# Holding back the value sums of every third step in a streamed attention kernel

## The chip, the cores and the metric

The kernel runs on one core of one Trainium2 chip. Times are device microseconds. The time of the kernel is the median of its runs; one further execution was taken with the profiler on, and its own time is given beside its span.

## The reference

Two transformer layers on 2048 rows of 256 features, 16 heads of 16. The first layer splits the rows into two halves: each attends to itself, then each to the other half, then an MLP with gelu. The second layer attends to all 2048 rows with a mask, then to a context of 1601 rows, then an MLP with relu. All four attentions are of this kind:

```
scores = jnp.einsum('bhqd,bhkd->bhqk', q, k) / jnp.sqrt(jnp.float32(hd))
if mask is not None:
    scores = jnp.where(mask == 0, jnp.float32(-1000000000.0), scores)
attn = jax.nn.softmax(scores, axis=-1)
out = jnp.einsum('bhqk,bhkd->bhqd', attn, v)
```

## The kernel before

**Units.** The four attentions are stages 0 to 3 of one stream. A unit is one block of 512 queries with one group of 4 heads; there are 68. A unit's keys come in tiles of 128. For each tile there are two steps, one for each pair of heads: 16 steps a unit in stages 0 and 1, 16 or 32 in the masked stage 2, 26 in stage 3; 1440 steps in all, 928 of them in stages 0, 1 and 3.

**A step** (`stream`, the loop at L1194). In this order PE is given:
- maxima of the next unit (`take_maxima`, L1200, from `maxima`): scores with queries on the partitions (L860, two matmuls that use 64 rows of the array each) into a score tile, which DVE reduces to the maximum (L875; L868 where there's a mask). About one such pair a step in stages 0 and 1; 32 for the 26 steps of a unit in stage 3.
- without a mask, the value sums that are due (L1201 to L1203): one entry of the list `pending`.
- the weights of this step (`second[s2]()`, L1204, from `weights_of`): scores with keys on the partitions (L938), minus the maxima (L945), in the masked stage the mask as well (L953), into a score tile; ACT takes exp of it into a tile `e` (L958).
- with a mask, the value sums come only now (L1205).
- `after(step)`: items with a delay (turning the maxima into rows, L899 to L904; dividing by the sums), transfers, and one piece of the background work.

**Value sums** (`values_of`). For each tile four matmuls (L975; the trace shows each as two) add `V` times `e` into a sum tile `m_ps`, each for one head in 32 columns of the array. The first and the last tile of a unit are summed whole, 512 queries wide, and leave an empty entry (`None`) in the list for the step after; every other tile is summed in two halves of 256 queries, one a step. So there are as many entries as steps. A unit's entries are put on the list in its fourth step (`s2 == 3`), and one is taken in each step; the last three are taken in the first three steps of the next unit. When those are through, `copy_sums` takes the sums out (L1007).

**Tiles.** Score tiles `s_ps` are two PSUM banks each, and there are three (`big_ps`, L107), used in turn by maxima and weights. The sum tiles m0 and m1 are one bank each; the small products of other work use the one that is not in use. `e` has five buffers (`EB`, L55).

**What sets the order.** The order on every engine is the order in which the program issues, fixed when it is built. Projections, MLPs and norms of the blocks run as generators (`chain_self` and so on) in the list `background`: each `yield` gives a number of steps to wait, and the first entry's due time is `background[0][1]`, in steps of `now[0]`. `before` and `after` advance them a piece at a time when they are due.

Of the kernel before, what the change touches and what calls it, by code (L numbers as in the profile page):

```python
# [66 lines left out]
def slot_rows(st, slot):  # L67
    return sum(key_rows(st, n) for n in KEYS[st][slot])


def slots_of(st, b):

    return ((b // 2,), (1 - b // 2,), (0, 1), (0, 1))[st]
# [3 lines left out]
def two_layers(ctx: ExitStack, tc: tile.TileContext, a: dict, out: bass.AP):  # L77
# [585 lines left out]
    now = [0]  # L663
# [30 lines left out]
    def want(*place):  # L694
        waiting.extend((kind, *place) for kind in ("keys", "values"))
# [186 lines left out]
    def negated(u):  # L882

        neg = sb.tile([P, TPB, 2, 2], F32, tag="neg", bufs=2, name="neg")
        nc.vector.tensor_reduce(
            neg.rearrange("p t c i -> p (t c i)"),
            u["pm"].rearrange("p t c i n -> p (t c i) n"), AX.X, ALU.max, negate=True,
        )
        v = negpad.rearrange("p t (c x) -> p t c x", c=2)
        nc.vector.tensor_copy(v[:, :, :, 0:3:2], neg)  # L890
        nc.vector.tensor_tensor(
            v[:, :, :, 1:4:2], neg, v[:, :, :, 0:3:2].bitcast(F32), ALU.subtract
        )

    def as_rows(u):

        m = one_ps()
        for qt in range(TPB):
            nc.tensor.matmul(  # L899
                m[:, qt * P : (qt + 1) * P], lhsT=negpad[:, qt, :], rhs=identR,  # L900
                start=True, stop=True,
            )
        u["nm"] = sb.tile([P, BLK], F32R, tag="nm", bufs=2, name="nm")
        nc.scalar.copy(u["nm"], m)  # L904
        if "part" in u:

            t = sb.tile([P, 2, 4 * BLK // P], F32, tag="mh", bufs=2, name="mh")
            for j in range(4):
                for h in range(2):
                    r = 64 * (j // 2) + 2 * (j % 2) + h  # L910
                    nc.sync.dma_start(
                        t[PH * j : PH * (j + 1), h, :], u["nm"][r : r + 1, :].bitcast(F32)
                    )

            def add():
                n = u["minus"] = part_tile(u, "minus")
                nc.vector.tensor_tensor(n, t[:, 0, :], t[:, 1, :], ALU.add)

            later.append([4, add, False])
# [180 lines left out]
    def stream(stages):  # L1100

        units = []
        for st in stages:
            for b in ORDER[st]:
                blocks[st, b] = {}
                if (st, b) == (2, SPLIT):
                    units += [
                        {"st": st, "b": b, "g": g, "slots": (slot,), "part": slot}
                        for slot in range(2) for g in range(NG)
                    ]  # L1110
                else:
                    units += [
                        {"st": st, "b": b, "g": g, "slots": slots_of(st, b)} for g in range(NG)
                    ]
        for i, u in enumerate(units):
            u["i"] = i

        columns: list = []
        at = 0
        for u in units:  # L1120
            steps = [(slot, kt) for slot in u["slots"] for kt in range(-(-slot_rows(u["st"], slot) // P))]
            if u["st"] == 2 and u["g"] == 0:
                columns += [
                    (at + 2 * n - COLUMNS, u["b"], slot, kt) for n, (slot, kt) in enumerate(steps)
                ]
            u["start"], u["steps"] = at, 2 * len(steps)
            at += 2 * len(steps)

        todo: list = []
        for u, w in zip(reversed(units), [*reversed(units[:-1]), None]):  # L1130
            tiles = maxima(u)
            n = len(tiles)
            begin, length = (w["start"], w["steps"]) if w else (-n, n)
            for k in range(n - 1, -1, -1):
                due = begin + k * length / n - AHEAD
                if u.get("part") == 1 and u["g"] == 0:

                    due = begin + (n - 1) * length / n - AHEAD - (n - 1 - k) * SPACING
                todo.append([min(due, todo[-1][0] - SPACING) if todo else due, u, tiles[k]])

        def take_maxima(step):
            while todo and todo[-1][0] <= step:
                _, u, f = todo.pop()
                f()
                if not todo or todo[-1][1] is not u:
                    all_maxima(u)

        def all_maxima(u):
            negated(u)
            later.append([3, lambda: as_rows(u), True])  # L1150
            if u.get("part") == 0 and u["g"] == NG - 1:
                want(2, 1, 1)

        def before():

            if unfinished and background and not background[0][2] and background[0][1] <= now[0]:
                if not advance(background[0]):
                    background.pop(0)

        def after(step):  # L1160

            now[0] += 1
            due = [x for x in later if x[0] <= 0]
            later[:] = [[x[0] - 1, *x[1:]] for x in later if x[0] > 0]
            for x in due:
                x[1]()
            turned = any(x[2] for x in due)
            while columns and columns[0][0] <= step:
                mask_columns(*columns.pop(0)[1:])
                turned = True  # L1170
            load_ready()
            soon = any(x[0] <= 0 and x[2] for x in later)
            soon = soon or (columns and columns[0][0] <= step + 1)
            if background and background[0][1] <= now[0]:
                if not background[0][2] or not (turned or soon):
                    if not advance(background[0]):
                        background.pop(0)

        streaming[0] = True
        for u in units[:2]:  # L1180
            load_queries(u)
        for step in range(math.floor(todo[-1][0]), 0):
            small[0] = 1
            before()
            take_maxima(step)
            after(step)
        pending: list = []
        step = 0
        for u in units:
            i = u["i"]  # L1190
            masked = u["st"] == 2
            small[0] = i % 2
            second = weights_of(u)
            for s2 in range(len(second)):  # L1194
                before()
                if s2 == 3:
                    pending += values_of(u)
                if s2 == 1 and i + 2 < len(units):
                    load_queries(units[i + 2])
                take_maxima(step)  # L1200
                f = pending.pop(0) if pending else None  # L1201
                if f and not masked:
                    f()  # L1203
                second[s2]()  # L1204

                if f and masked:
                    f()
                after(step)
                step += 1
                if s2 == 2:  # L1210
                    small[0] = (i + 1) % 2
                if s2 == 2 and i:
                    w = units[i - 1]
                    copy_sums(w)
                    part = w.get("part")
                    if part is None:
                        later.append([3, lambda w=w: invert(w), False])
                        later.append([6, lambda w=w: divide(w), False])
                    elif part == 1:
                        v = units[i - 1 - NG]  # L1220
                        later.append([3, lambda w=w, v=v: compare(w, v), False])
                        later.append([4, lambda w=w, v=v: invert_both(w, v), False])
                        later.append([7, lambda w=w: (fetch_first(w), divide(w)), False])
                    if w["g"] == NG - 1 and part != 0:
                        chain_after(w)
        small[0] = len(units) % 2
        for f in pending:
            if f:
                f()
        for x in later:  # L1230
            x[1]()
        flush((0, 1))
        streaming[0] = False
        w = units[-1]
        copy_sums(w)
        invert(w)
        divide(w)
        chain_after(w)
        while background:
            if not advance(background[0]):  # L1240
                background.pop(0)
        flush((None,))
# [92 lines left out]
```

## Time and profile before

| what | us |
|---|---|
| median of 3 runs (3391.25 to 3396.46) | 3392.64 |
| the profiled execution | 3403.53 |
| its span | 3401.7 |
| before the stream's first step (to 131) | 131.0 |
| stage 0 (131 to 632.5): PE busy 465.9 | 501.5 |
| stage 1 (632.5 to 1271.4): PE busy 578.2 | 638.9 |
| stage 2, masked (1271.4 to 2510): PE busy 1191.4 | 1238.6 |
| stage 3 (2510 to 3325): PE busy 766.4 | 815.0 |
| the end (from 3325) | 76.7 |

The stages are cut where the first L938 of each starts. PE's granted clock is 0.97 to 0.99 in all four stages. A line of the timeline gives the start, the duration, engine, source line, operation, what it writes and reads, shapes, a count, and in brackets the idle time of the engine before it with what ended it. PE is the matmul, PEld the weight load; "64*128" is the part of the array that a matmul uses, rows by columns. A matmul's recorded duration reaches past the start of the next one, since matmuls are pipelined, so what a piece of PE's work costs is read from the starts.

### The profile page before, as it was taken

The page shows a single profiled execution, that of the slowest core. Times are in us where ns is not written, and L with a number is a line of the kernel's source. Part 1 is how long each engine was busy: PE and PEld are TensorE (multiplying, and loading weights), DVE is VectorE, ACT ScalarE, POOL GpSimd, SP SyncE. Part 2 cuts the span into 40 slices and gives each one's busy share as a digit, 9 for nine tenths or more (in the row PEclk, how much of TensorE's full clock was granted, in tenths as well). Part 3 has the DMA queues.
Part 4 walks back from the last instruction along what each step waited for, and adds up shares of the span by engine and source line. Part 5 has one row for each costly group of instructions (what it writes and reads, how often), then busy time and mean ns, then how long its engine had stood idle before and what let it go on. Part 6 is the DMA issues. An engine that isn't in the chain of part 4 may idle for free.

```text
span 3401.7 us, 56761 instructions
## 1 busy us (share of the span) xinstructions
PE 3113.2 (92%) x22592; PEld 1362.0 (40%) x22592; DVE 2120.7 (62%) x3858; ACT 1713.7 (50%) x1868; POOL 404.6 (12%) x344
## 2 busy tenths in 40 slices
PE   4799999998999889898999999999999999999995
PEld 2334444444444433333333333343334444444433
DVE  2676766764646455366767777767656747657541
ACT  1265655655545445343555555554546646546461
POOL 0001101101010121104023012201010011110102
PEclk8799999999999999899999999999999999999997
DMA  5652162160204121343111001102241100000000
GB/s 177 140 105 65 36 117 65 48 128 24 65 18 114 32 84 37 94 100 107 51 39 51 15 20 58 32 17 55 49 87 43 26 10 26 25 18 26 10 14 16
DMA packets 162362, 191.20 MB, mean 56 GB/s; under 512 B 82584, under 2 KB 95520, under 8 KB 162096
## 3 DMA queue, kind: packets, MB, share of 16 engines
q1 hardware_dynamic: 162096, 187.57, 22.3%
q8 instruction: 178, 2.92, 0.4%
q14 instruction: 88, 0.72, 0.1%
HBM read 129.91 MB, written 48.46 MB: 52 GB/s over the span
## 4 chain that ended last, share of the span: by engine, by line
PE 51%; DVE 5%; ACT 4%; DMA 2%; SPq 2%; POOL 1%; issue 1%; ACTq 0%; POOLq 0%; DVEq 0%
PE m_ps L975 13%; PE s_ps L938 8%; PE s_ps L860 8%; PE s_ps L953 7%; PE s_ps L945 6%; ACT e L958 3%; PE m_ps L515 2%; DVE s_ps L868 2%; PE m_ps L535 2%; DVE pm L875 1%; PE m_ps L460 1%; DMA raw<-in_mask 1%; PE m_ps L385 1%; DVE t L328 1%; PE m_ps L415 1%
## 5 line engine op out<-in xcount | busy, mean ns | idle before, releaser
L958 ACT ACTIVATE e<-s_ps 128x1024 f32<-128x1024 f32 (+1 forms) x1440 | 1468.1, 1025 | 1375.0 <-PE s_ps L945 794.8
L875 DVE TENSOR_REDUCE pm<-s_ps 128x2 f32<-128x1024 f32 (+3 forms) x1024 | 1120.9, 1106 | 534.7 <-PE s_ps L860 530.2
L975 PE MATMUL m_ps<-e,V 128*32 128x256 f32 (+2 forms) x10432 | 903.6, 418 | 7.3 <-ACT hT L354 4.4
L868 DVE CUSTOM_DVE_ANT_0 s_ps<-s_ps,bias 128x512 f32<-128x512 f32 x1024 | 712.8, 701 | 295.4 <-PE s_ps L860 161.6
L860 PE MATMUL s_ps<-kT,q 64*128 64x512 f32 (+3 forms) x3072 | 676.6, 443 | 111.8 <-ACT e L958 51.1
L938 PE MATMUL s_ps<-q,kT 64*128 64x512 f32 (+1 forms) x2880 | 677.3, 466 | 51.8 <-ACT e L958 28.4
L945 PE MATMUL s_ps<-nm,sel 64*128 64x512 f32 (+1 forms) x2880 | 575.2, 395 | 0.1
L860 PEld LDWEIGHTS s_ps<-kT,q 64*128 64x128 f32 x3072 | 294.1, 186 | 528.1 <-issue 301.1
L938 PEld LDWEIGHTS s_ps<-q,kT 64*128 64x128 f32 (+1 forms) x2880 | 270.5, 184 | 496.6 <-issue 241.0
L975 PEld LDWEIGHTS m_ps<-e,V 128*32 128x32 f32 (+1 forms) x10432 | 206.9, 108 | 433.6 <-issue 415.3
L953 PE MATMUL s_ps<-biasT,ident 128*128 128x512 bf16 x1024 | 311.4, 386 | 0.0
L1053 POOL TENSOR_TENSOR oT<-oT,rd_rows 64x512 f32<-64x512 f32 x64 | 81.7, 1277 | 1904.8 <-DMA rd_rows<-rd_dr 1491.1
L945 PEld LDWEIGHTS s_ps<-nm,sel 64*128 64x128 f32 (+1 forms) x2880 | 275.2, 187 | 12.1 <-ACT nm L904 0.8
L805 POOL TENSOR_SCALAR bias<-raw 128x512 bf16<-128x512 int32 x64 | 123.1, 1924 | 266.4 <-DMA raw<-in_mask 256.4
L868 DVE DVE_READ_ACCUMULATOR2_ANT pm<- 128x1 f32 x1024 | 144.9, 141 | 0.0
L953 PEld LDWEIGHTS <-ident 128*128 128x128 bf16 x1024 | 58.4, 97 | 187.8 <-issue 187.8
L393 DVE SCALAR_TENSOR_TENSOR lo<-m_ps,qkb,hi 128x512 fp32r<-128x512 f32 (+2 forms) x56 | 41.1, 734 | 137.3 <-ACT hi L392 94.3
L535 PE MATMUL m_ps<-w_mlp,hid 128*128 128x256 f32 x448 | 111.4, 405 | 11.9 <-ACT hid L534 11.9
L385 PE MATMUL m_ps<-hT,w_qk 128*128 128x512 f32 (+2 forms) x224 | 109.8, 613 | 9.3 <-DVE lo L393 8.8
L515 PE MATMUL m_ps<-hT,w_mlp 128*128 128x512 f32 x224 | 111.0, 618 | 1.1 <-ACT hT L354 1.1
L535 PEld LDWEIGHTS m_ps<-w_mlp,hid 128*128 128x128 f32 x448 | 86.3, 200 | 36.5 <-ACT hid L534 16.3
L415 PE MATMUL m_ps<-w_v,hT 128*128 128x256 f32 (+1 forms) x212 | 58.0, 420 | 21.8 <-DVE lo L393 21.4
(106 smaller groups left out, 1220.9 us busy)
## 6 DMA issues: line engine op xcount, KB each, us to landing
q<-q_dr SPq DMA_DIRECT2D x544, 64.0 KB
kT<-k_dr SPq DMA_DIRECT2D x192, 128.0 KB
raw<-in_mask SPq DMA_DIRECT2D x64, 256.0 KB
q_dr<-hi SPq DMA_DIRECT2D x32, 256.0 KB
q_dr<-lo SPq DMA_DIRECT2D x32, 256.0 KB
oT<-sums SPq DMA_DIRECT2D x256, 32.0 KB
rd_rows<-rd_dr SPq DMA_DIRECT2D x64, 128.0 KB
v_dr<-v SPq DMA_DIRECT2D x14, 544.0 KB
```

The lines of the kernel that those rows point to most:

```text
L385: nc.tensor.matmul(m[:, :n], lhsT=wqk[:, k, w, c, :], rhs=hT[:, k, :n], start=k == 0, stop=k == 1)
L515: nc.tensor.matmul(m, lhsT=w1[k][:, f * P : (f + 1) * P], rhs=hT[:, k, :], start=k == 0, stop=k == 1,)
L535: nc.tensor.matmul(m[:, q2 * D : (q2 + 1) * D], lhsT=hid[f][:, qt * P : (qt + 1) * P], rhs=w2[f // 4][:, f % 4, :], start=f == 0, stop=f = ...
L805: nc.gpsimd.tensor_scalar(bias_rows[b, slot, qt][:, j * BLK : (j + 1) * BLK], raw, 0.0, MASKED, ALU.is_equal, ALU.mult,)
L860: nc.tensor.matmul(s[:, h, :nn], lhsT=u["q"][64 * h : 64 * h + 64, i, qt * P : (qt + 1) * P], rhs=kT[g][slot][64 * h : 64 * h + 64, i, c : ...
L868: nc.vector.tensor_tensor_reduce(out=s[:, h, :], in0=s[:, h, :], in1=bias_rows[b, slot, qt][:, c : c + nn], scale=1.0, scalar=-3.0e38, op0 ...
L875: nc.vector.tensor_reduce(u["pm"][:, qt, :, i, n], s[:, :, :nn], AX.X, ALU.max)
L938: nc.tensor.matmul(s[:r, h, :], lhsT=kT[g][slot][64 * h : 64 * h + 64, i, kt * P : kt * P + r], rhs=u["q"][64 * h : 64 * h + 64, i, :], st ...
L945: nc.tensor.matmul(s[:r, h, :], lhsT=sel[64 * h : 64 * h + 64, i, :r], rhs=u["nm"][64 * h : 64 * h + 64, :], start=False, stop=not masked,)
L953: nc.tensor.matmul(s[:, h, :], lhsT=ident16, rhs=bias_columns[b, slot, kt], start=False, stop=True,)
L958: nc.scalar.activation(e[:r], s[:r], AF.Exp, scale=SCALE)
L975: nc.tensor.matmul(u["av"][PH * j : PH * (j + 1), cut], lhsT=V[g][slot][:r, kt * GW + j * VW : kt * GW + j * VW + PH], rhs=u["e"][n, j % 2 ...
```

## The change

In stages without a mask, a step whose number is a multiple of three leaves its entry on the list if no piece of background work is due (`quiet`) and at least four steps of the unit are done (`s2 >= 4`). The count `owed` grows by one each step; a step that sums takes as many entries as are owed. So in three steps it is none, then two, then one. If a piece is due, or in the masked stage, or in a unit's first four steps, everything that is owed is summed. The order of maxima, sums and weights in a step is unchanged.

```
         pending: list = []
+        owed = 0
         step = 0
...
                 take_maxima(step)
-                f = pending.pop(0) if pending else None
-                if f and not masked:
-                    f()
+                owed += 1
+
+
+                quiet = not (background and background[0][1] <= now[0])
+                sums = []
+                if masked or not quiet or step % 3 or s2 < 4:
+                    sums = [f for f in pending[:owed] if f]
+                    del pending[:owed]
+                    owed = 0
+                if not masked:
+                    for f in sums:
+                        f()
                 second[s2]()
 
-                if f and masked:
-                    f()
+                if masked:
+                    for f in sums:
+                        f()
                 after(step)
```

## The prediction

> **What bounds the kernel now.** I read the page first: busy time, then the chain that ended last, then the waits of PE, and at last the timeline of the stages that the change touches.
>
> ```profile
> PE 3113.2 (92%) x22592; PEld 1362.0 (40%) x22592; DVE 2120.7 (62%) x3858; ACT 1713.7 (50%) x1868; POOL 404.6 (12%) x344
> ...
> PE 51%; DVE 5%; ACT 4%; DMA 2%; SPq 2%; POOL 1%; issue 1%; ACTq 0%; POOLq 0%; DVEq 0%
> ```
>
> PE leads both. ACT and DVE are far from full, so only their latency can matter, not their throughput. PE's own waits, longest first:
>
> ```profile
> PE s_ps L860 <- ACT e L958: 51.1, 84, 1.2
> ...
> PE s_ps L938 <- ACT e L958: 28.4, 94, 0.9
> ```
>
> The dearest wait is not for data: L860 (maxima scores) reads nothing that L958 (exp) writes. It waits until exp has emptied the score tile that it is to write over; there are three. Now an ordinary stretch of stage 0, PE alone (start us, duration us; idle before it in brackets):
>
> ```profile
> 338.57 0.50 PE L938 MATMUL s_ps<-q,kT 64*128 64x512 f32 x2
> 338.91 0.39 PE L945 MATMUL s_ps<-nm,sel 64*128 64x512 f32 x2
> 339.15 0.39 PE L860 MATMUL s_ps<-kT,q 64*128 64x512 f32 x2
> 339.47 0.64 PE L975 MATMUL m_ps<-e,V 128*32 128x256 f32 x8
> 340.04 0.50 PE L938 MATMUL s_ps<-q,kT 64*128 64x512 f32 x2
> ```
>
> From one L938 to the next, a "row", is 1.47 us with PE never waiting. The same kernel already has rows without values, since the first and last tile of a unit are summed whole and leave the next step empty. Here is one, with what follows:
>
> ```profile
> 360.31 0.50 PE L938 MATMUL s_ps<-q,kT 64*128 64x512 f32 x2
> ...
> 360.65 0.40 PE L945 MATMUL s_ps<-nm,sel 64*128 64x512 f32 x2
> ...
> 360.88 0.40 PE L860 MATMUL s_ps<-kT,q 64*128 64x512 f32 x2
> ...
> 361.12 0.39 PE L938 MATMUL s_ps<-q,kT 64*128 64x512 f32 x2
> ...
> 361.14 1.94 ACT L958 ACTIVATE e<-s_ps 128x1024 f32<-128x1024 f32 x2 [0.91 <-PE s_ps L945]
> 361.35 0.40 PE L945 MATMUL s_ps<-nm,sel 64*128 64x512 f32 x2
> ...
> 362.22 0.49 PE L860 MATMUL s_ps<-kT,q 64*128 64x512 f32 x2 [0.48 <-ACT e L958]
> ...
> 362.65 0.64 PE L975 MATMUL m_ps<-e,V 128*32 128x256 f32 x8
> ...
> 363.22 0.50 PE L938 MATMUL s_ps<-q,kT 64*128 64x512 f32 x2
> ```
>
> The empty row takes 0.81 us, but the next L860 then stands: its tile was filled by the L938 of 360.31, whose exp starts at 361.14 and ends 1.02 us later, and it starts at 362.22, 1.91 us after that L938. So the two rows together take 2.91 us with one half tile, almost what two ordinary rows take with two (2.93). In the timeline all 21 such places of stages 0 and 1 where no piece of other work lies between have that L860 1.90 to 1.92 us after the L938. This is the change's pattern, made by the kernel itself.
>
> **What the Trainium skill says.** "TensorEngine Tiling (Array Packing)", section Tiling Modes: changing the tiling mode drains the array. The trace agrees: a group of four L975 matmuls of 256 columns follows another 0.24 us later, but L938, in the other mode, 0.33 us later. "PSUM — Partial Sum Buffer", section Specifications (TRN2): eight banks of 2 KiB a partition. Three score tiles of two banks and two sum tiles of one fill them, so there's no fourth score tile; the waits above agree. "Perfetto Trace Analysis", section Optimization Strategy: the same gap recurring on the engine that should be full can mean that there's no room for the next tile. The 0.48 us before L860 is such a gap.
>
> **The change part by part.** Walking the new loop, 196 of 928 unmasked steps hold their sums back (103 in stage 3, 93 in stages 0 and 1). In 10 the held entry is an empty one, so 186 places really change. Built, PE's order shows just that: runs of eight L975 where four stood, one instruction stream otherwise; DVE, ACT, POOL and SP keep theirs. A moved half tile issues four matmuls (eight in the trace), no DMA; no queue but PE's is passed. No tile, load or exp is added.
>
> *Switches saved.* A row without its half tile takes 0.81 for 1.47: −0.66. The half tile costs two more groups in the next run: 2 × 0.24 = +0.48. After scores instead of values, L945 follows its L938 in 0.23, not 0.34: −0.11. Together −0.29 us a place, −54 us for 186, if nothing waits.
>
> *Wait added.* The second L860 comes 0.81 + 0.23 + 0.23 = 1.27 us after the first L938, and can't start before 1.91. Behind it on PE stand 16 value matmuls and the next L938; DVE's maximum of that tile starts late too. A weight load that waits isn't ahead of time: L860 to L975 is then 0.43, not 0.32. With a double run of 3 × 0.24 + 0.33 = 1.05 the two rows take 1.91 + 0.43 + 1.05 = 3.39 for 2.93: +0.46. By the other way, 2.91 above and 0.48 more is 3.39 too. Afterwards nothing is late: the second exp ends near 2.9, before its tile is wanted at 3.9; the wait isn't paid back, since PE has no slack in ordinary rows.
>
> I sorted the 186 places by the two rows that they stand in before (durations from the timeline):
> - 66 with two ordinary rows: +0.46, +30 us.
> - 27 in stage 3 with a row of two L860 pairs. 16 where that row loses its values: it waits for exp until 1.91 with or without them, so their 0.48 is simply added, +7.7. In 7 the row that gets them has two pairs: 1.91 + 0.30 (second pair) + 0.30 + 1.05 = 3.56 for 3.33, +1.6. In 4 the next row waits as well, so some 0.3 of the 0.48 stays, +1.2.
> - 17 with one pair each and a row of 1.90 (L938 waits there for the exp just before). In 9 the second row's wait swallows the loss: 0. In 8: 0.47, +3.8.
> - 34 with a row over 2.05 (after an empty row, a DMA or a table load): between −0.29 and +0.46; mostly cover is there; I take +0.1, +3.4.
> - 23 with the turned maxima (L899) in a row: 0.79 us longer, so L860 arrives after 1.91 and the wait vanishes; I take −0.25 of the −0.29: −5.8.
> - 8 at the end with fewer maxima: −0.2, −1.6.
> - 11 beside pieces: −0.29 to +0.46; I take 0.
>
> Sum: 30 + 10.5 + 3.8 + 3.4 − 5.8 − 1.6 = +40 us. The profiled execution took 3403.5 (span 3401.7 and 1.8 around), 0.3% over the median of 3392.6; it would become 3443.8, and the median 3432.9. I name 3433, 1.2% slower.
>
> **The rivals.**
> *Switches win (faster).* The drain is saved everywhere, and the wait at L860 only takes the place of one that came soon after anyway: the 84 and 94 waits above show that score tiles are often late. It decides by the wait a place: under 0.29 us it's a gain, over it a loss. At none it is 3392.6 − 54 = 3339. Against it: 0.64 us (1.91 − 1.27) at every empty row, and 66 ordinary places with no wait to displace.
> *Cover is wider than I see (no change).* If the waits are inherited by the next ones (DMA, L938 behind exp), the 66 places cost nothing and the total is some +10; if the 27 do too, nothing: 3393 to 3411.
> *All stall.* If the 34, 23 and 11 lose 0.46 like the rest, 68 × 0.46 = 31 instead of −2.4: +74, 3466; a further knock-on on chains of pieces would add to it.
> That the change does nothing is excluded by PE's order.
>
> **How the numbers follow.** Forecast 0.70, its own range from the two unknown kinds (45 places, −16 to +17 about what I took) and some 5 us of spread: 3412 to 3455. Inherited waits 0.10, switches win 0.12, all stall 0.08. From 3398 to 3464 keeps eight in ten. A measurement of this kernel can tell about 0.2% (7 us) from no change. Faster than that: 0.11; within it: 0.06; slower: 0.83.
>
> **What would show it.** Right: L860 behind ACT e L958 grows from 84 waits and 51 us to about 180 and 95 (idle shows some 0.48 for a loss of 0.64), and L938 behind it by some 8 us; L975's busy time hardly moves; ACT and DVE do the same work over a longer span; the masked stage keeps its 1239 us; stage 3 grows by some 23 us. Wrong: double runs that follow L860 in 0.32 us with no idle before it, so two rows in 2.64. Then exp is not what L860 waits for.

## The result, and the profile after

The changed kernel takes 3423.7 us (median of 13 runs, 3409.7 to 3430.0) beside 3397.1 for the kernel before on the same chips (13 runs): ratio 1.0073, 95% interval 1.0059 to 1.0086. The change costs 0.7%, some 25 us; 1.2% (40 us) had been forecast.

The page after: busy time and the chain that ended last.

```profile
PE 3078.9 (90%) x22592; PEld 1376.9 (40%) x22592; DVE 2117.8 (62%) x3858; ACT 1704.3 (50%) x1868; POOL 404.6 (12%) x344
...
PE 50%; DVE 6%; ACT 4%; DMA 2%; issue 1%; SPq 1%; POOL 1%; ACTq 0%; POOLq 0%; DVEq 0%
```

PE is busy for 34 us less than before and yet the span is 6 us longer, so PE stands idle for 40 us more. The busy time falls because two single runs of L975 are recorded with 0.64 us each and a double run with 1.07, 0.21 less, which makes 39 us at 186 places. The waits of PE, for the same two instructions as before:

```profile
PE s_ps L860 <- ACT e L958: 81.5, 162, 1.2
PE s_ps L938 <- ACT e L958: 39.6, 78, 1.0
```

L860's wait for exp has gone from 84 times and 51.1 us to 162 times and 81.5 us, L938's from 28.4 to 39.6 us. Here is one held-back place in stage 0 (step 138), PE alone; in the kernel before its two rows took 1.46 and 1.47 us.

```profile
393.09 0.50 PE L938 MATMUL s_ps<-q,kT 64*128 64x512 f32 x2 [0.38 <-ACT e L958]
393.43 0.40 PE L945 MATMUL s_ps<-nm,sel 64*128 64x512 f32 x2
393.67 0.39 PE L860 MATMUL s_ps<-kT,q 64*128 64x512 f32 x2
393.89 0.40 PE L938 MATMUL s_ps<-q,kT 64*128 64x512 f32 x2
394.12 0.39 PE L945 MATMUL s_ps<-nm,sel 64*128 64x512 f32 x2
395.00 0.50 PE L860 MATMUL s_ps<-kT,q 64*128 64x512 f32 x2 [0.49 <-ACT e L958]
395.44 1.07 PE L975 MATMUL m_ps<-e,V 128*32 128x256 f32 x16
396.44 0.50 PE L938 MATMUL s_ps<-q,kT 64*128 64x512 f32 x2
```

The row without values takes 0.80 us; then L860 stands until 395.00, 1.91 us after the L938 of 393.09, the same 1.91 that the empty rows before had. The double run (16 records of L975) comes behind it, and the two rows take 3.35 us.

By stages, from the first L938 of each to that of the next (in stage 3 to its last), the kernel grows by 3.0, −0.4 and −3.0 us in stages 0, 1 and 2 and by 12.9 us in stage 3. The profiled executions differ by less than the medians (3409.7 and 3403.5), and their granted clocks differ with them: 0.973 after and 0.968 before, and 0.005 of 3405 us are 17 us (an estimate). That is why the places are compared by pairs of rows below, and kernels by runs.

### The profile page after: what moved, and what is told of

The parts are those of the page before. It is cut to its first block, busy times and chain, and to the rows that moved or that the text cites. A ratio compares the mean times of both kernels' runs of the same rounds, so it can differ in the third digit from the quotient of the medians.

```text
span 3407.8 us, 56762 instructions
## 1 busy us (share of the span) xinstructions
PE 3078.9 (90%) x22592; PEld 1376.9 (40%) x22592; DVE 2117.8 (62%) x3858; ACT 1704.3 (50%) x1868; POOL 404.6 (12%) x344
## 4 chain that ended last, share of the span: by engine, by line
PE 50%; DVE 6%; ACT 4%; DMA 2%; issue 1%; SPq 1%; POOL 1%; ACTq 0%; POOLq 0%; DVEq 0%
PE m_ps L975 14%; PE s_ps L860 8%; PE s_ps L938 8%; PE s_ps L953 7%; PE s_ps L945 5%; ACT e L958 4%; PE m_ps L515 2%; DVE s_ps L868 2%; PE m_ps L535 2%; DVE pm L875 1%; DMA raw<-in_mask 1%; PE m_ps L460 1%; PE m_ps L385 1%; DVE t L328 1%; POOL bias L805 1%
## 5 line engine op out<-in xcount | busy, mean ns | idle before, releaser
L958 ACT ACTIVATE e<-s_ps 128x1024 f32<-128x1024 f32 (+1 forms) x1440 | 1458.6, 1024 | 1399.7 <-PE s_ps L945 820.6
L875 DVE TENSOR_REDUCE pm<-s_ps 128x2 f32<-128x1024 f32 (+3 forms) x1024 | 1118.5, 1107 | 556.8 <-PE s_ps L860 554.9
L975 PE MATMUL m_ps<-e,V 128*32 128x256 f32 (+2 forms) x10432 | 864.7, 415 | 6.8 <-ACT hT L354 4.4
L860 PE MATMUL s_ps<-kT,q 64*128 64x512 f32 (+3 forms) x3072 | 680.8, 446 | 140.8 <-ACT e L958 81.5
L938 PE MATMUL s_ps<-q,kT 64*128 64x512 f32 (+1 forms) x2880 | 669.0, 460 | 70.0 <-ACT e L958 39.6
L945 PE MATMUL s_ps<-nm,sel 64*128 64x512 f32 (+1 forms) x2880 | 573.1, 393 | 0.1
L860 PEld LDWEIGHTS s_ps<-kT,q 64*128 64x128 f32 x3072 | 291.8, 185 | 576.3 <-issue 303.8
L938 PEld LDWEIGHTS s_ps<-q,kT 64*128 64x128 f32 (+1 forms) x2880 | 269.9, 184 | 464.2 <-issue 203.4
L975 PEld LDWEIGHTS m_ps<-e,V 128*32 128x32 f32 (+1 forms) x10432 | 226.9, 109 | 419.7 <-issue 373.2
L945 PEld LDWEIGHTS s_ps<-nm,sel 64*128 64x128 f32 (+1 forms) x2880 | 274.4, 186 | 13.5 <-ACT nm L904 0.8
L393 DVE SCALAR_TENSOR_TENSOR lo<-m_ps,qkb,hi 128x512 fp32r<-128x512 f32 (+2 forms) x56 | 41.1, 734 | 135.6 <-ACT hi L392 99.2
L385 PE MATMUL m_ps<-hT,w_qk 128*128 128x512 f32 (+2 forms) x224 | 111.5, 622 | 8.6 <-DVE lo L393 8.1
L515 PE MATMUL m_ps<-hT,w_mlp 128*128 128x512 f32 x224 | 111.0, 618 | 1.0 <-ACT hT L354 1.0
L392 ACT ACTIVATE hi<-m_ps,qkb 128x512 fp32r<-128x512 f32 (+2 forms) x56 | 37.8, 675 | 75.4 <-PE m_ps L385 58.5
```

Of the source, the lines that this page charges most:

```text
L385: nc.tensor.matmul(m[:, :n], lhsT=wqk[:, k, w, c, :], rhs=hT[:, k, :n], start=k == 0, stop=k == 1)
L515: nc.tensor.matmul(m, lhsT=w1[k][:, f * P : (f + 1) * P], rhs=hT[:, k, :], start=k == 0, stop=k == 1,)
L860: nc.tensor.matmul(s[:, h, :nn], lhsT=u["q"][64 * h : 64 * h + 64, i, qt * P : (qt + 1) * P], rhs=kT[g][slot][64 * h : 64 * h + 64, i, c : ...
L875: nc.vector.tensor_reduce(u["pm"][:, qt, :, i, n], s[:, :, :nn], AX.X, ALU.max)
L938: nc.tensor.matmul(s[:r, h, :], lhsT=kT[g][slot][64 * h : 64 * h + 64, i, kt * P : kt * P + r], rhs=u["q"][64 * h : 64 * h + 64, i, :], st ...
L945: nc.tensor.matmul(s[:r, h, :], lhsT=sel[64 * h : 64 * h + 64, i, :r], rhs=u["nm"][64 * h : 64 * h + 64, :], start=False, stop=not masked,)
```

## The experiments

All 186 places were followed in the traces: the two rows in which the held step lies, against the same two rows of the kernel before.

### The change at the ordinary places alone

The condition `step % 3` is replaced by a list of 66 step numbers, those of the prediction's first kind (the list, `PLACES`, is left out here).

```
-                if masked or not quiet or step % 3 or s2 < 4:
+                if masked or not quiet or step not in PLACES or s2 < 4:
```

> The change at the 66 places alone that lie in two ordinary rows (one pair of maxima, no piece, no turned maxima, nothing late in the kernel before); in the other 120 the sums stay one a step. Theory: 66 x 0.41 us = +27 us, ratio 1.008, as much as all 186 together, whose rest cancels out. Rival (the loss is spread over all places, or comes from a lower granted clock): 66 / 186 of 25 us, +9 us, ratio 1.003.

Measured: 3420.1 us, ratio 1.0052 (1.0032 to 1.0072), some 18 us. In the trace the 66 pairs of rows are 0.42 us longer at the median and 27.7 us together; the other 120 places are as before (medians within 0.02 us in every kind). The rival's 1.003 is the lower edge of the interval, but the trace leaves nothing to it: the loss sits in these places, and at nearly the price of the sum. The clock of its runs was 0.969 to 0.974, that of the kernel before beside it 0.966 to 0.972, so a lower clock is not what makes it slow.

### Sums ahead of the maxima

In a step that sums twice, the value matmuls go ahead of the maxima scores.

```
-                take_maxima(step)
                 owed += 1
...
+                early = not masked and len(sums) > 1
+                if early:
+                    for f in sums:
+                        f()
+                take_maxima(step)
-                if not masked:
+                if not masked and not early:
```

> The same 186 double runs, but in a step that sums twice the value matmuls are issued ahead of the maxima scores (L860) and not behind them. Theory (the loss is PE standing at L860 until exp has emptied the score tile): the double run fills the time that L860 had to wait, so two ordinary rows take some 0.81 + 0.23 + 0.32 + 1.05 + 0.23 = 2.64 us for 2.93 before, -0.29; the places that wait for another exp still lose. Sum over the kinds of places about -33 us, ratio 0.990 to the kernel before. Rival 1 (the loss lies in the double runs themselves, or in their late sums): the order doesn't matter, +25 us, ratio 1.007. Rival 2 (the wait is only moved to the next L938): near 1.000.

Measured: 3402.4 us, ratio 1.0014 (1.0005 to 1.0023). The order matters, so the double run isn't dear by itself: 20 of the 25 us are gone, and at the 66 ordinary places +0.42 has become +0.05 at the median (27 us together have become 12). L860's wait for exp is back at 83 times. But nothing is gained, where 33 us had been expected. PE's other waits show why, here those that have grown over the kernel before (18.7 us and 21 times, 8.7 us and 22 times there):

```profile
PE s_ps L860 <- DVE pm L875: 30.6, 55, 2.2
...
PE s_ps L938 <- DVE pm L875: 25.4, 45, 2.0
```

The maxima scores now come later, so their reduction on DVE (1.23 us each, L875) does, and it's the reduction that keeps the next score tile. My expectation had looked at one reader of the tiles, exp, and not at the other. Besides, the weights of L938 are loaded only as it starts when it has waited, and L945 then follows in 0.34 us, not 0.23 (349.68 to 350.02 in its trace), which takes part of the saving.

### Every second step

`step % 2` for `step % 3`, so that two half tiles of the same tile are summed every second step, once with the maxima first, and once with the sums first (the edit above in addition).

```
-                if masked or not quiet or step % 3 or s2 < 4:
+                if masked or not quiet or not (step % 2 == 1) or s2 < 4:
```

> The change, but every second step holds its half tile back and the next one sums the whole tile: 298 double runs for 186, maxima ahead of the sums as in the change. Theory: each place costs what it did in the change, so 298 / 186 x 25 = +40 us, ratio 1.012. Rival (the loss comes from the uneven pattern of none, two, one): an even pattern of none, two loses less than the change, and with 298 x 0.29 us of switches saved it would be faster than before, down to 0.975.

> Both: every second step holds back, and the sums of a double run are issued ahead of the maxima scores. Theory: the saving of e1 times 298 / 186, about -53 us, ratio 0.984, since every place now saves its switches and L860 comes after exp has ended. Rival 1 (double runs cost by themselves): slower than before, as the kernel with every second step and maxima first. Rival 2 (the value matmuls now come too early for the exp that they read): PE waits at L975 for L958 and the gain is gone, 1.000.

Measured, maxima first: 3421.1 us, ratio 1.0064 (1.0051 to 1.0077). It's a loss again and not the gain of the rival, but it's half of the 40 us that I had scaled up from the number of places. The places don't wait less often: L860 waits for exp 202 times, 118 more than in the kernel before, 0.40 a place, for 0.42 in the change. At the 24 of the 66 ordinary places that it holds as well it is +0.42 us, the price in the change. But this kernel holds odd steps alone, and in the change itself the 98 places with an odd step cost 4.3 us together, the 88 with an even one 20.9. I had scaled the mean of both.

Measured, sums first: 3436.0 us, ratio 1.0113 (1.0097 to 1.0130). My expectation of −53 us has failed altogether. The longest wait of PE is now another:

```profile
PE s_ps L938 <- DVE pm L875: 82.3, 153, 1.3
```

In the kernel before that line had 8.7 us. With the sums ahead in every second step, two maxima come close behind each other, and L938, which is to write over the tile of the first, waits for its reduction. So PE waits for one reader of the tiles or for the other, and its own order chooses which.

### Without maxima

L860 and L875 are left out in the unmasked stages, and a constant is written where the maxima would stand: this part of the computation is missing from these three kernels, so the tiles go to exp alone. Once with the step loop of the kernel before, once with that of the change, once with every second step.

```
                 u["pm"] = sb.tile([P, TPB, 2, 2, len(chunks)], F32, tag="pm", bufs=2, name="pm")
+                if not masked:
+                    nc.gpsimd.memset(u["pm"], 40.0)
+            if not masked:
+                return
```

> The kernel before without the maxima scores and their reduction in the stages without a mask (L860 and L875 are left out there; a constant stands for the maxima, so the softmax isn't shifted rightly). It is the base for the next kernel. Each ordinary row shrinks to 1.24 us, as in the last unit of the kernel before: some 1000 pairs of maxima of 0.23 us, about -220 us, ratio 0.93; all theories say the same.

> The changed kernel with the same part left out. Score tiles now go to exp alone, and one is wanted again three rows later, so the wait that the change brought has no place. Theory: the 186 double runs save their switches, as the 8 places with fewer maxima did (-0.27 each): -50 us against the kernel before without maxima. Rival 1 (the loss is of the double runs themselves): +25 us against it. Rival 2 (PE is bound by exp once maxima are gone): no difference.

> Without maxima in the unmasked stages, as e6 and e7 (that part is left out), and every second step holds back, so that a double run is always the two halves of one tile and reads only exps that are two steps old: 298 double runs. Theory: of the 186 of e7 half saved 0.34 us and half nothing, because a double run over two tiles reads the exp of the step just before and waits for it; here all save, 298 x -0.34 = -100 us against the kernel before without maxima, ratio to the kernel before 0.901. Rival (it is the half of the places with other rows around them that can't save): the mean of e7, 298 x -0.16 = -48 us, ratio 0.916.

Measured: 3160.3 us with the step loop of the kernel before (ratio 0.9304, 0.9287 to 0.9320), 3144.4 with the change (0.9250, 0.9236 to 0.9264), 3100.0 with every second step (0.9127, 0.9114 to 0.9139). With the maxima gone, L942 and L864 (L938 and L860 elsewhere) wait for exp for 4.5 us in all with the change, where it was 121.1 us. The same change then gains 16 us, and that of every second step 60. That's the mechanism shown from the other side: the switches are worth saving where no score tile is late.

The change gained less than the 50 us expected. In its trace the 98 places with an odd held step are 0.345 us shorter at the median and the 88 with an even one 0.00, 34 us together. Of these 16 are left in the runs, whose granted clock was lower too: 0.955 to 0.957 for 0.959 to 0.960, and 0.004 of 3150 us are some 13 us (an estimate). Two places of stage 3, steps 1170 and 1173, of which the second is the better one (here L942, L949, L962 and L979 are what L938, L945, L958 and L975 are elsewhere):

```profile
2646.84 0.50 PE L942 MATMUL s_ps<-q,kT 64*128 64x512 f32 x2
...
2647.41 0.39 PE L942 MATMUL s_ps<-q,kT 64*128 64x512 f32 x2
...
2647.97 1.42 PE L979 MATMUL m_ps<-e,V 128*32 128x256 f32 x16
...
2648.76 0.15 PEld L979 LDWEIGHTS m_ps<-e,V 128*32 128x32 f32 x6 [0.22 <-ACT e L962]
2649.32 0.19 PEld L942 LDWEIGHTS s_ps<-q,kT 64*128 64x128 f32 x2 [0.41 <-issue]
```

```profile
2650.55 0.50 PE L942 MATMUL s_ps<-q,kT 64*128 64x512 f32 x2
...
2651.12 0.39 PE L942 MATMUL s_ps<-q,kT 64*128 64x512 f32 x2
...
2651.68 1.07 PE L979 MATMUL m_ps<-e,V 128*32 128x256 f32 x16
2652.68 0.50 PE L942 MATMUL s_ps<-q,kT 64*128 64x512 f32 x2
```

In the first the run takes 1.35 us to the next L942, in the second 1.00. The weight load in its midst waits for exp: a run that goes over from one tile to the next reads the exp of the step just before, one of the two halves of one tile doesn't. The kernel with every second step holds back before whole tiles alone, and there 297 places are 0.344 us shorter at the median, 82 us together, which rules out the rival's −0.16. Of these 60 are left in the runs; the granted clock was 0.951 to 0.952 in its runs, 0.959 to 0.960 in those of the base, and 0.008 of 3100 us are some 25 us (an estimate again). Where the clock is lower can be read from the traces: at a granted clock of 0.50 PE spends 52 us of stages 0 and 1 in the kernel before, and 119, 147 and 143 us in these three. There PE now has long waits for other work: in the first of the three kernels it waits three times for 13.5 to 15.0 us at L460, in the kernel before at most 3.6. What another order of that work would give was not tried.

### Held back beside other work

The condition turned round: hold back only if a piece of background work is due or the turned maxima follow.

```
-                if masked or not quiet or step % 3 or s2 < 4:
+                turn = any(x[0] <= 0 and x[2] for x in later)
+                if masked or (quiet and not turn) or owed > 1 or s2 < 4:
```

> The condition turned round: a step holds its half tile back only if a piece of background work is due or the turned maxima come right after it (never two steps in a row, never in a unit's first four steps, not in the masked stage), 106 double runs, maxima ahead of the sums as in the change. Theory (the loss is PE standing at L860 for an exp that is not yet through): the matmuls of the piece stand between the two score tiles, so L860 comes after exp has ended and the switches saved are left, up to 106 x -0.29 = -31 us; pieces without matmuls leave some places waiting, so -20, ratio 0.994. Rival (double runs cost by themselves, some 25 / 186 = 0.13 us each): +14 us, ratio 1.004.

Measured: 3386.9 us, ratio 0.9956 (0.9941 to 0.9972): faster than both kernels, and 92 of its 106 double runs stand where the change has none. PE's wait at L860 is what it was in the kernel before:

```profile
PE s_ps L860 <- ACT e L958: 51.1, 84, 1.2
```

By the work that stands between: the 44 places with turned maxima (L899) are 0.22 us shorter at the median, 15 between two pieces of the MLP (L515) 0.32, 7 between two of the value projection (L415) 0.35. But 15 places between two pieces of the query and key projection (L385) are 0.43 longer. Its next piece waits for DVE and ACT to take the last one out of PSUM, and the value sums had covered that: at step 86 PE now stands there for 0.73 us. PE's wait at L385, in the kernel before and in this one:

```profile
PE m_ps L385 <- DVE lo L393: 8.8, 8, 1.6
```

```profile
PE m_ps L385 <- DVE lo L393: 18.1, 19, 1.9
```

4 places beside L343 are 0.43 us longer as well; there L938 waits for L875.

So a last kernel with a list of 94 places: those of this kernel and of the change that the traces show shorter, none beside L385.

> The change's double runs at 94 listed places alone: those of the kernel that holds back beside other PE work, and those of the change, whose two rows were over 0.1 us shorter in the traces (turned maxima, pieces of MLP and projection, few maxima; none of the query and key projections L385, where the exp waits on ACT behind another copy). Theory: the places keep what they showed, 94 x -0.29 = -27 us, ratio 0.992. Rival (single traces, chance of one execution): the mean over such places without choosing, -0.10 each, -9 us, ratio 0.997.

Measured: 3375.1 us, ratio 0.9945 (0.9930 to 0.9961). Its places keep −0.29 us at the median and −19.4 us together; the runs show some 19. That is short of the 27 us expected. Its ratio is the lowest with the whole computation, but its interval overlaps that of the last kernel, so which of the two is faster isn't shown. That the exp waits behind a copy on ACT beside L385, as I had expected, isn't what the trace shows: PE's wait for L393 is.

## Why the prediction was right, and where its size was off

The direction, the mechanism and the range hold; the cost is 25 us for 40. That 3423.7 lies so near to the 3433 named is in part chance: the kernel before took 3397.1 us in 13 runs, 4.5 more than in the three that were counted from.

*What bounds: right.* PE, held up where none of the three score tiles is free. The empty rows of the kernel before told the pattern and its price: L860 1.91 us after the L938 there, and the same at the place shown after.

*Switches saved: right, with a term missing.* −0.29 us a place was the estimate. Measured are −0.30 at the median of the places with turned maxima, and −0.344 without maxima where the double run stays in one tile. Where it goes over from one tile to the next, the kernel without maxima saves nothing (0.00): the run waits for the exp of the step just before, which the estimate didn't have. With the maxima, at ordinary places, this doesn't show: +0.42 for the 42 even steps and for the 24 odd ones.

*Wait added: right, a little too dear.* +0.46 was the estimate for ordinary rows, +0.42 is measured. I had priced a double run as 3 × 0.24 + 0.33 = 1.05 us; it takes 1.00 (395.44 to 396.44), since the second group of a run follows the first in 0.24, but the third and the fourth follow in 0.22.

*The kinds of places*: the sum was 40 us by these terms, and is 25 by the traces of before and after.

| kind | places | predicted, us | measured, us (median of one) |
|---|---|---|---|
| two ordinary rows | 66 | +30 | +27.2 (+0.42) |
| row with two L860 pairs loses its values | 16 | +7.7 | +6.0 (+0.43) |
| row with two pairs gets them | 7 | +1.6 | +1.9 (+0.20) |
| two pairs, next row waits as well | 4 | +1.2 | −0.9 (−0.33) |
| one pair each, a row of 1.90 | 17 | +3.8 | +1.1 |
| a row over 2.05 | 34 | +3.4 | −0.7 (−0.11) |
| turned maxima | 23 | −5.8 | −5.1 (−0.30) |
| fewer maxima | 8 | −1.6 | −2.1 (−0.27) |
| beside pieces | 11 | 0 | −2.2 (−0.33) |

The signs of the large terms hold. What made it 15 us too much were 3 us at the ordinary places and some 12 us elsewhere, above all in places that I had taken as waiting or as neutral. Of the 17, the 4 with two waiting rows lost nothing (+0.01 each for +0.47), since a second row that waits for exp anyway hides the double run in that wait; there I had let the wait of the first row decide. Of the 4 with two pairs, where the next row waits as well, 3 even save 0.33 us each. The 11 had been taken as neutral, and 7 of them save their switches.

Two lines of the table say less than they seem to. The −5.1 us of the turned maxima is near the forecast by averaging: the 14 odd steps are −0.34 us at the median and the 9 even ones +0.01, where −0.25 had been taken for each. And of the 34 places, 13 lie, before or after, in a stretch with a granted clock of 0.50, so they range from −1.58 to +1.30 us by chance (−1.5 together); the other 21 make +0.8 us, where +2.1 had been taken.

*What would show it.* L860's waits went to 162 and 81.5 us for some 180 and 95, L938's grew by 11 us for 8, stage 3 by 12.9 us for 23 (its places by 18.6, while its granted clock was 0.99 for 0.97). The masked stage kept its time but for 3 us. One sign failed: L975's busy time was hardly to move, and it fell from 903.6 to 864.7 us, since a double run is recorded shorter than two single ones.

*The rivals.* Switches win: true at single places and in the kernels without maxima, not in the whole. Cover wider than seen: of the 15 us that are missing it can have taken up to 12. All stall: not so.

## What to carry to other kernels

Before work is moved out of a gap between two users of a buffer, take the lifetime of that buffer (here 1.91 us from the scores to the end of exp) and set it against the time that PE needs to come round without that work: if that time is shorter than the lifetime, the move turns work into idle time. Take such filler away where other work already stands between the two users, and leave it where nothing else does: there it is needed. And a buffer with two kinds of readers has to be reckoned for both, since easing the one brings out the other.

## What the runs showed of the hardware

- An engine's order alone moved 20 us: the same instructions with the value runs ahead of the maxima scores instead of behind them.
- The spread of the runs of one kernel goes with the granted clock: 3409.7 us at 0.973 and 3430.0 at 0.967 for the changed kernel, 20 us for 0.006 of 3420.
- These means are made of two values. In every trace the granted clock is 1.00 or 0.50, in intervals of 3.41 us; at 0.50 are 220 us of the kernel before and 186 of the changed one. In the streamed stages of the kernel before, 20 intervals at 1.00 were followed by one at 0.50: PE's recorded busy time was up to 0.56 of the interval in 19 of them, and 0.69 in one. Of the 879 that were followed by another at 1.00 none was under 0.56. In the changed kernel it was up to 0.51 in 18, and not under 0.55 in the other 890. So in these traces waits that crowd into one such interval are followed by a slow one: from 716.31 to 719.72 us of the kernel before PE was busy for 1.85 us of 3.41, and the next interval ran at 0.50. The two rows of step 297, which lie there, took 5.59 us, and 4.03 in the changed kernel, where they ran at 1.00.
- Without maxima the granted clock was lower in all runs, 0.959 to 0.960, and lower still with double runs, 0.955 to 0.957 and 0.951 to 0.952, though PE was as busy over the whole (91%, 90% and 90%). With maxima double runs did not lower it (0.967 to 0.973 after the change, 0.969 to 0.973 with every second step).
